# One signal per round, a fourth buffer of split rows, and one wait per block in a two-layer graph network

## The chip, the cores and the metric

The kernel runs on one core of one Trainium2 chip. The metric is the device time of one execution in microseconds. A core has five engines with queues of their own: TensorE (PE; PEld is its weight load), VectorE (DVE), ScalarE (ACT), GpSimd (POOL) and SyncE (SP). An engine works through its queue in order, and engines wait for each other through semaphores. In this kernel SyncE issues nearly all plain transfers and GpSimd the indirect ones (gathers).

## The reference

A graph of 12500 nodes with 256 features and 200000 edges, sorted by destination; destinations are skewed to low node numbers. Two layers of mean aggregation, an output product, a residual and a normalization:

```python
def _sage_conv(x, src, dst, W_l, b_l, W_r):
    msgs = x[src]
    agg = jax.ops.segment_sum(msgs, dst, num_segments=N_NODES)
    deg = jax.ops.segment_sum(jnp.ones((src.shape[0],), x.dtype), dst, num_segments=N_NODES)
    mean = agg / jnp.maximum(deg, 1.0)[:, None]
    return mean @ W_l + b_l + x @ W_r

h = jax.nn.relu(_sage_conv(x, src, dst, W1_l, b1, W1_r))
h = jax.nn.relu(_sage_conv(h, src, dst, W2_l, b2, W2_r))
return layernorm(x + h @ W3 + b3)
```

All in float32, weights 256 x 256. (A second routine, `by_sorting`, serves inputs that do not fit the first; it is built in but not run here.)

## The kernel before

The destinations are cut into blocks of 128 nodes, 98 of them (`NB`). Edges are aggregated in two ways.

The low, much hit destinations (five groups of 256 in layer 1, seven in layer 2) go the **dense** way. `count` builds a matrix of how often each source stands before each destination of the group: VectorE compares (`pick`, L661; `low`, L665; `aft`, L671), TensorE multiplies (L706, L710) into one of three PSUM buffers `count_ps`, ScalarE copies into `counts` (L712). `product` (L628) then multiplies these counts with all rows of the table. The rows are held in DRAM as three bfloat16 parts each, `x3_d` in layer 1 and `h3_d` in layer 2. For every pair of row blocks SyncE loads one buffer `rows` (L635, 384 KB; three buffers), and TensorE does 12 matmuls on it (L638). Before that, `split_rows` (L622) makes the parts of x: a load of `split_sb`, then in turns ScalarE (L617, L619) and VectorE (L618, L620), then a store (L626).

The other edges go by **gathers**. A round takes four tiles of 128 edges. GpSimd gathers their source rows with four indirect transfers (L243) into one of four buffers `got`; TensorE multiplies the four with 0/1 matrices, 32 destinations each, into four 32-row strips of one PSUM tile (L254, in the order 3, 2, 1, 0); ScalarE copies the tile (`some`, L259). One step later `summed` adds it at the right place of a ring of sums in SBUF (L265 on TensorE, L277 on VectorE; L270 and L273 for the degrees in layer 1). A gather has to wait until the strip that last read its buffer is done, four rounds back. There are 516 rounds, 269 in layer 1 and 247 in layer 2.

When a block's sums are complete, the **block** runs in pieces: its own rows are loaded (L833) and transposed (L839, after L886 for the degrees in layer 1; copied out by L842), then `sage` (L859) makes the two products (L863 with the sums, L865 with the own rows) into one of two PSUM buffers `block_ps`, and VectorE adds (L868, L869) into the one buffer `own`; ScalarE applies the relu (L871). In layer 1 the result is stored whole (L896) and in three parts (L617 to L620 again, L899). In layer 2 it is transposed, multiplied with W3 (L921), added to x (`z`, L923), normalized and stored (L934). Where the sums came from the ring, ScalarE clears that part of it (L894 in layer 1, L913 in layer 2).

The order on TensorE and GpSimd is the order in which the program is written: `layer` (L562) steps through the rounds, lets at most two blocks be under way, a piece of one at least two turns after the piece before, and fills each third of a round with dense and counting work up to a planned cost. VectorE, ScalarE and SyncE are ordered by the tile framework's scheduler, which puts an instruction in its queue when its operands and buffers are there by its own reckoning. The framework also makes all semaphores: an instruction signals if another engine has to wait for it. An instruction holds few waits of its own; further ones stand in separate instructions ahead of it, which do nothing else. `tc.add_manual_dep(later, earlier, ...)` adds a wait by hand.

Of the kernel before, what the change touches and what calls it, by code (L numbers as in the profile page):

```python
# [7 lines left out]
F32 = mybir.dt.float32  # L8
F16 = mybir.dt.float16
BF16 = mybir.dt.bfloat16  # L10
# [7 lines left out]
ACT = mybir.EngineType.Activation  # L18
PE = mybir.EngineType.PE
POOL = mybir.EngineType.Pool  # L20

P = 128
LN_EPS = 1e-5
# [24 lines left out]
def by_runs(  # L48
# [27 lines left out]
    nc = tc.nc  # L76
    N, D = x.shape
    E = src.shape[0]
    NB = -(-N // P)
    NC = D // P  # L80
    G, W = 4, 32
# [44 lines left out]
    h_d = dram.tile([NB * P, D], F32, name="h_d")  # L126
# [46 lines left out]
    part_pool = ctx.enter_context(tc.tile_pool(name="part_ps", bufs=1, space=PSUM))  # L173
    sum_pool = ctx.enter_context(tc.tile_pool(name="sum_ps", bufs=1, space=PSUM))

    REGS = 8

    class Values:
# [5 lines left out]
        def at(self, i):  # L184
            if i not in self.have:
                a = i - self.i0
                n = min(REGS, self.row.shape[1] - a)
                _, v = nc.values_load_multi_w_load_instructions(
# [27 lines left out]
    class Gathers:  # L216
# [20 lines left out]
        def gathered(self, i):  # L237

            (gr, r), g = self.rounds[i], got[i % NGOT]
            t0, n = groups[gr]  # L240
            for j in range(G):
                e = t0 + j * n + r - C0 * P
                nc.gpsimd.indirect_dma_start(  # L243
                    out=g[:, j, :D], out_offset=None, in_=self.table,
                    in_offset=bass.IndirectOffsetOnAxis(ap=src_t[:, e:e + 1], axis=0))
            if i + AHEAD < len(self.rounds):
                self.chosen[i + AHEAD] = select(*self.rounds[i + AHEAD], self.second)
            one, two = self.chosen.pop(i)
            if r == 0:
                self.part_ps = part_pool.tile([P, D + 1], F32, name="part_ps")  # L250
            part_ps, width = self.part_ps, self.width

            for j in reversed(range(G)):
                nc.tensor.matmul(part_ps[j * W:(j + 1) * W, :width], lhsT=one[:, j],  # L254
                                 rhs=g[:, j, :width], start=r == 0, stop=r == n - 1)
            if r < n - 1:
                return None
            some = chosen_pool.tile([P, D + 1], F32, name="some", bufs=2)
            nc.scalar.copy(some[:, :width], part_ps[:, :width])  # L259
            return gr, some, two  # L260
# [18 lines left out]
    with tc.tile_pool(name="setup", bufs=1) as su, \  # L279
# [140 lines left out]

        ctx.enter_context(tc.manual_schedule(engines={PE, POOL}))
        gathers_1 = Gathers(x, False)
# [20 lines left out]
        start = su.tile([P, HC], F32, name="start")  # L443
# [8 lines left out]
        for g, (c0, c1) in enumerate(spans):  # L452
            n = c1 - c0
# [46 lines left out]
        for t in range(0, HT, 32):  # L500
            n = min(32, HT - t)
# [28 lines left out]
    w1l_sb, w1r_sb = weight(w1l, "w1l_sb"), weight(w1r, "w1r_sb")  # L530
    w2l_sb, w2r_sb, w3_sb = weight(w2l, "w2l_sb"), weight(w2r, "w2r_sb"), weight(w3, "w3_sb")

    biases = consts.tile([P, 3, D], F32, name="biases")
# [3 lines left out]
    zeros = zero.unsqueeze(2).to_broadcast([P, NC, P])  # L537
# [16 lines left out]
    work = ctx.enter_context(tc.tile_pool(name="work", bufs=2))  # L554
# [73 lines left out]
    def product(g, table3, c_sb):  # L628

        ps = dense_pool.tile([P, NC, DN], F32, name="dense_ps")  # L630
        nc.tensor.matmul(ps, lhsT=zeros_b, rhs=c_sb[:, :NC, :DN], start=True, stop=False)
        for b in range(NB):
            if b % 2 == 0:
                rows = work.tile([P, 2, 3, D], BF16, name="rows", bufs=3)
                nc.sync.dma_start(rows, table3[:, b:b + 2])  # L635
            for k in range(3):
                for c in range(NC):
                    nc.tensor.matmul(ps[:, c], lhsT=rows[:, b % 2, k, c * P:(c + 1) * P],  # L638
                                     rhs=c_sb[:, b, :DN],
                                     start=False, stop=b == NB - 1 and k == 2 and c == NC - 1)  # L640
            yield COST_DENSE
        d_sb = work.tile([P, NC, DN], F32, name="d_sb", bufs=1)
        nc.scalar.copy(d_sb, ps)
        yield d_sb
# [180 lines left out]
        return whole  # L825


    def load_rows(table, n_rows, b, name):
        t = work.tile([P, D], F32, name=name)
        n = min(P, n_rows - b * P)  # L830
        if n < P:
            nc.vector.memset(t, 0.0)
        nc.sync.dma_start(t[:n], table[b * P:b * P + n, :])  # L833
        return t

    def transposed(t, ps, name, more=0):

        for c in range(NC):
            nc.tensor.transpose(ps[:, c], t[:, c * P:(c + 1) * P], ident)  # L839
        s = work.tile([P, NC * P + 1], F32, name=name)  # L840
        n = NC * P + more
        nc.scalar.copy(s[:, :n], ps.rearrange("p c l -> p (c l)")[:, :n])  # L842
        return s[:, :NC * P].rearrange("p (c l) -> p c l", l=P), s[:, NC * P:]

    def ring(b):
# [10 lines left out]
                nc.vector.tensor_add(d, d, degs[:, RN:])  # L856
                nc.scalar.copy(degs[:, RN:], zeros[0:1, 0])

    def sage(own_t, b, agg, wl, wr, bias, name):  # L859

        ps = block_pool.tile([P, 2, D], F32, name="block_ps")
        for c in range(NC):
            nc.tensor.matmul(ps[:, 0], lhsT=agg[:, c], rhs=wl[:, c], start=c == 0, stop=c == NC - 1)  # L863
        for c in range(NC):
            nc.tensor.matmul(ps[:, 1], lhsT=own_t[:, c], rhs=wr[:, c], start=c == 0,  # L865
                             stop=c == NC - 1)
        own = work.tile([P, D], F32, name="own", bufs=1)
        nc.vector.tensor_add(own, ps[:, 1], bias)  # L868
        nc.vector.scalar_tensor_tensor(own, ps[:, 0], rdeg[:, b:b + 1], own, op0=OP.mult, op1=OP.add)  # L869
        h = work.tile([P, D], F32, name=name)  # L870
        nc.scalar.activation(h, own, AF.Relu)  # L871
        return h, own

    def turned():
        t = block_pool.tile([P, 2, D], F32, name="block_ps")
        return t.rearrange("p two (a l) -> p (two a) l", l=P)

    def first_block(b, agg=None):
        x_sb = load_rows(x, N, b, "x_sb")
        of_ring = agg is None  # L880
        yield True
        ps = turned()
        if of_ring:
            overlap(b, True)
            agg, deg_row = ring(b)
            nc.tensor.matmul(ps[:, NC, 0:1], lhsT=deg_row, rhs=ones[0:1, 0:1], start=True, stop=True)  # L886
        x_t, deg = transposed(x_sb, ps, "own_t", int(of_ring))
        if of_ring:
            nc.vector.tensor_scalar(deg, deg, 1.0, None, op0=OP.max)
            nc.vector.reciprocal(rdeg[:, b:b + 1], deg)  # L890
        yield True
        h, own = sage(x_t, b, agg, w1l_sb, w1r_sb, biases[:, 0], "h")
        if of_ring:
            nc.scalar.copy(agg, zeros)  # L894
            nc.scalar.copy(deg_row, zeros[0:1, 0])
        nc.sync.dma_start(h_d[b * P:(b + 1) * P, :], h)  # L896
        s = work.tile([P, 3, D], BF16, name="parts")
        exact(h, s, own)
        nc.sync.dma_start(h3_d[:, b], s)  # L899
        yield True  # L900

    def last_block(b, agg=None):
        h_sb = load_rows(h_d, NB * P, b, "h_sb")
        of_ring = agg is None
        yield True
        if of_ring:
            overlap(b, False)
            agg, _ = ring(b)
        h_t, _ = transposed(h_sb, turned(), "own_t")
        yield True  # L910
        h2, _ = sage(h_t, b, agg, w2l_sb, w2r_sb, biases[:, 1], "h")
        if of_ring:
            nc.scalar.copy(agg, zeros)  # L913
        x_sb = load_rows(x, N, b, "x_sb")
        yield True
        h2_t, _ = transposed(h2, turned(), "own_t")
        nc.vector.tensor_add(x_sb, x_sb, biases[:, 2])
        yield True
        y = block_pool.tile([P, 2, D], F32, name="block_ps")
        for c in range(NC):  # L920
            nc.tensor.matmul(y[:, 0], lhsT=h2_t[:, c], rhs=w3_sb[:, c], start=c == 0, stop=c == NC - 1)  # L921
        z = work.tile([P, D], F32, name="z")
        nc.vector.tensor_add(z, y[:, 0], x_sb)  # L923
        stats = work.tile([P, 6], F32, name="stats")
        nc.vector.bn_stats(stats, z)
        mv = work.tile([P, 2], F32, name="mv")
        nc.vector.bn_aggr(mv, stats)
        std = work.tile([P, 1], F32, name="std")
        nc.scalar.activation(std, mv[:, 1:2], AF.Sqrt, bias=eps)
        rstd = work.tile([P, 1], F32, name="rstd")  # L930
        nc.vector.reciprocal(rstd, std)
        nc.vector.tensor_scalar(z, z, mv[:, 0:1], rstd, op0=OP.subtract, op1=OP.mult)
        n = min(P, N - b * P)
        nc.sync.dma_start(out[b * P:b * P + n, :], z[:n])  # L934
        yield True
# [16 lines left out]
def by_sorting(  # L952
# [225 lines left out]

    REGS = 8

# [137 lines left out]
```

## Time and profile before

| | |
|---|---|
| three runs | 2904.64, 2908.94, 2911.25 us; median 2908.94 |
| the profiled execution | 2910.6 us, span 2908.8 us, mean granted TensorE clock 0.914 |
| busy | PE 2394.6 us (82%), POOL 2065.3 (71%), PEld 1632.6 (56%), DVE 1471.2 (51%), ACT 1253.6 (43%) |
| transfers | 676.44 MB, mean 233 GB/s |
| gathers L243 | 2064, of 0.95 us each in the median |
| dense matmuls L638 | 7056, 976.9 us busy |
| strips L254 | 2064 products in two passes, 359.7 us busy |

In the profile's lines `out<-in` are the program's tiles, `xN` is a count, and an arrow `<-` after an idle time or in a wait names who ended it. A line of waits reads: engine and instruction, whom it waited for, total us, number of times, longest. SPq is SyncE's queue; "issue" is time in which an engine waited for nothing that the profile shows. A line of the timeline starts with the start and the duration in us. Matmuls are pipelined and their ends are modelled, so busy times of PE overlap with each other.

### The profile page before, as it was taken

The numbers are of one execution on the slowest core, as the hardware profiler recorded it, in microseconds if no ns is written. First come the engines' busy times: TensorE is split into PE (matmuls) and PEld (weight loads), VectorE is DVE, ScalarE is ACT, GpSimd is POOL, SyncE is SP. The second block draws the span as 40 slices with busy tenths as digits, with TensorE's granted clock in tenths as the row PEclk, the third lists the DMA queues.
The fourth block names the chain that finished last, engine by engine and source line by source line (L and its number), as shares of the span: only waits on it lengthen the run. The fifth ranks groups of instructions, "written<-read, shape, count | busy, mean of one in ns | idle before, by whom it ended". The sixth has DMA issues, their size and how long they took to land.

```text
span 2908.8 us, 54100 instructions
## 1 busy us (share of the span) xinstructions
PE 2394.6 (82%) x18630; PEld 1632.6 (56%) x18630; DVE 1471.2 (51%) x4350; ACT 1253.6 (43%) x2702; POOL 2065.3 (71%) x2074
## 2 busy tenths in 40 slices
PE   3475755898998999999996677877889898899995
PEld 1132323565665666666764455555666666677774
DVE  6687764664554565566564124434323333444443
ACT  0422764675675676677673014444112122222222
POOL 5777764777777777777774777777777777777772
PEclk9676767998999999999998899889999999999998
DMA  4455668877877878767864677777989989888872
GB/s 124 128 174 164 198 188 271 260 232 235 277 228 247 273 227 292 248 215 225 251 203 124 214 246 231 219 220 230 296 284 305 299 287 291 276 265 266 266 251 71
DMA packets 408133, 676.44 MB, mean 233 GB/s; under 512 B 59659, under 2 KB 266537, under 8 KB 407849
## 3 DMA queue, kind: packets, MB, share of 16 engines
q1 hardware_dynamic: 303415, 400.51, 42.5%
q0 software_dynamic: 99072, 270.66, 30.5%
q8 instruction: 149, 2.44, 0.3%
q10 hardware_dynamic: 5362, 1.72, 0.3%
q14 instruction: 135, 1.11, 0.1%
HBM read 582.80 MB, written 89.87 MB: 231 GB/s over the span
## 4 chain that ended last, share of the span: by engine, by line
PE 54%; DMA 19%; POOL 8%; issue 7%; DVE 6%; ACT 4%; DVEq 0%; SPq 0%; ACTq 0%; POOLq 0%
PE dense_ps L638 19%; POOL got L243 8%; PE part_ps L254 7%; PE block_ps L863 6%; DMA got<-h_d,src_t 5%; PE count_ps L706 5%; PE block_ps L865 5%; PE sum_ps L265 4%; DMA x_sb<-in_x_dram 3%; DMA rows<-h_d 3%; DMA rows<-x_d 3%; PE block_ps L839 2%; PE block_ps L921 2%; DMA split_sb<-in_x_dram 2%; PE sum_ps L270 2%
## 5 line engine op out<-in xcount | busy, mean ns | idle before, releaser
L243 POOL DMA_INDIRECT got<-in_x_dram,src_t x1076 | 1116.7, 1038 | 446.5 <-issue 274.2
L243 POOL DMA_INDIRECT got<-h_d,src_t x988 | 946.4, 958 | 343.1 <-issue 285.3
L638 PE MATMUL dense_ps<-counts,rows 128*128 128x256 bf16 x7056 | 976.9, 279 | 51.3 <-DMA rows<-h_d 27.7
L712 ACT CAST counts<-count_ps 128x392 f32 (+2 forms) x1052 | 717.6, 682 | 290.2 <-PE count_ps L710 174.0
L638 PEld LDWEIGHTS <-rows 128*128 128x128 bf16 x7056 | 671.3, 100 | 287.5 <-issue 88.6
L254 PE MATMUL part_ps<-got,one 128*32 128x257 f32 (+1 forms) x4128 | 359.7, 422 | 192.1 <-DMA got<-h_d,src_t 123.0
L706 PE MATMUL count_ps<-pick,low 128*128 128x392 bf16 (+2 forms) x1052 | 343.4, 354 | 57.0 <-ACT counts L712 27.0
L661 DVE TENSOR_SCALAR pick<-steps,key_t 128x686 bf16<-128x686 f16 (+2 forms) x748 | 301.4, 413 | 127.6 <-PE count_ps L706 110.2
L201 DVE TENSOR_TENSOR one<-lo_t,lane_b 128x128 f32<-128x128 bf16 x516 | 149.1, 289 | 372.7 <-PE part_ps L254 370.5
L259 ACT COPY some<-part_ps 128x257 f32<-128x257 f32 (+1 forms) x361 | 136.1, 377 | 431.4 <-PE part_ps L254 428.2
L254 PEld LDWEIGHTS part_ps<-got,one 128*32 128x32 f32 x4128 | 85.9, 111 | 323.5 <-issue 176.4
L265 PE MATMUL sum_ps<-two,some 128*128 128x128 f32 x1444 | 238.2, 290 | 0.2 <-DVE sums L277 0.2
L265 PEld LDWEIGHTS sum_ps<-two,some 128*128 128x128 f32 x1444 | 205.0, 201 | 20.5 <-issue 8.7
L277 DVE TENSOR_TENSOR sums<-sums,sum_ps 128x256 f32 x361 | 148.4, 411 | 132.6 <-PE sum_ps L265 101.9
L868 DVE TENSOR_TENSOR own<-block_ps,biases 128x256 f32<-128x256 f32 x196 | 83.0, 423 | 230.9 <-PE block_ps L865 230.2
L706 PEld LDWEIGHTS <-low 128*128 128x128 bf16 x1052 | 101.8, 100 | 152.3 <-DVE pick L661 54.2
L842 ACT COPY own_t<-block_ps 128x256 f32<-128x256 f32 (+1 forms) x294 | 110.0, 375 | 123.7 <-PE block_ps L839 121.2
L871 ACT ACTIVATE h<-own 128x256 f32<-128x256 f32 x196 | 81.4, 415 | 179.3 <-DVE own L869 179.2
L665 DVE TENSOR_TENSOR low<-low_t,lane_b 128x512 bf16<-128x512 bf16 x187 | 127.9, 684 | 21.1 <-PE count_ps L710 20.5
L710 PE MATMUL count_ps<-aft,low 128*128 128x98 bf16 x614 | 131.9, 215 | 0.0
L863 PE MATMUL block_ps<-w1l_sb,sums 128*128 128x256 f32 x352 | 113.9, 452 | 2.1 <-DVE sums L277 1.8
L863 PE MATMUL block_ps<-w2l_sb,sums 128*128 128x256 f32 x336 | 104.1, 437 | 11.3 <-DVE sums L277 11.1
(180 smaller groups left out, 2495.1 us busy)
## 6 DMA issues: line engine op xcount, KB each, us to landing
rows<-h_d SPq DMA_DIRECT2D x343, 384.0 KB
rows<-x_d SPq DMA_DIRECT2D x245, 384.0 KB
count_d<-counts SPq DMA_DIRECT2D x28, 896.0 KB
counts<-count_d SPq DMA_DIRECT2D x28, 896.0 KB
x_sb<-in_x_dram SPq DMA_DIRECT2D x194, 128.0 KB
x_d<-parts SPq DMA_DIRECT2D x98, 192.0 KB
h_d<-parts SPq DMA_DIRECT2D x98, 192.0 KB
got<-in_x_dram,src_t POOLq DMA_INDIRECT x1076
```

The source lines that it names most:

```text
L201: nc.vector.tensor_tensor(one, lo[:, a:a + n * (G - 1) + 1:n].unsqueeze(2).to_broadcast([P, G, W]), lane_b[:, :W].unsqueeze(1).to_broadcas ...
L243: nc.gpsimd.indirect_dma_start(out=g[:, j, :D], out_offset=None, in_=self.table, in_offset=bass.IndirectOffsetOnAxis(ap=src_t[:, e:e + 1], ...
L254: nc.tensor.matmul(part_ps[j * W:(j + 1) * W, :width], lhsT=one[:, j], rhs=g[:, j, :width], start=r == 0, stop=r == n - 1)
L259: nc.scalar.copy(some[:, :width], part_ps[:, :width])
L265: nc.tensor.matmul(sum_ps[:, c], lhsT=some[:, c * P:(c + 1) * P], rhs=two, start=True, stop=True)
L277: nc.vector.tensor_add(own, own, sum_ps[:, :NC])
L638: nc.tensor.matmul(ps[:, c], lhsT=rows[:, b % 2, k, c * P:(c + 1) * P], rhs=c_sb[:, b, :DN], start=False, stop=b == NB - 1 and k == 2 and ...
L661: nc.vector.tensor_scalar(r[:, :w * NB], steps[:, :w * NB], key_t[g][:, t - lo_g:t - lo_g + 1], None, op0=OP.is_equal)
L706: nc.tensor.matmul(ps[:, :(b - a) * NB], lhsT=s, rhs=r[:, a * NB:b * NB], start=True, stop=alone)
L712: nc.scalar.copy(to[:, :, bass.ds(n0 + a, b - a)], ps[:, :(b - a) * NB].rearrange("p (d s) -> p s d", s=NB))
L863: nc.tensor.matmul(ps[:, 0], lhsT=agg[:, c], rhs=wl[:, c], start=c == 0, stop=c == NC - 1)
L865: nc.tensor.matmul(ps[:, 1], lhsT=own_t[:, c], rhs=wr[:, c], start=c == 0, stop=c == NC - 1)
```

## The change

It has three named parts, and some that come with them.

- A round's four strips signal once. The first strip in order (strip 3) is made to wait for all four gathers of its round, so the others need no wait, and only the last strip's signal is used.
- A buffer `rows` is free for its next load when the first round's strips after its products are done, instead of the products themselves; there are four such buffers, not three. If those strips are not yet written when the load is, the load falls back on the wait that the framework finds.
- In `sage` the first product waits for the sums and for `own_t`, so that the four products signal once at the end; the ring is cleared after the last of them.
- The buffers: `own` has two instead of one, `z` shares them; `h_sb` shares the buffers of `split_sb`.

```diff
@@ Gathers.gathered
+            landing = []
             for j in range(G):
                 e = t0 + j * n + r - C0 * P
-                nc.gpsimd.indirect_dma_start(
+                rows = nc.gpsimd.indirect_dma_start(
                     out=g[:, j, :D], out_offset=None, in_=self.table,
                     in_offset=bass.IndirectOffsetOnAxis(ap=src_t[:, e:e + 1], axis=0))
+                landing.append(rows.ins.name)
...
             for j in reversed(range(G)):
-                nc.tensor.matmul(part_ps[j * W:(j + 1) * W, :width], lhsT=one[:, j],
-                                 rhs=g[:, j, :width], start=r == 0, stop=r == n - 1)
+                strip = nc.tensor.matmul(part_ps[j * W:(j + 1) * W, :width], lhsT=one[:, j],
+                                         rhs=g[:, j, :width], start=r == 0, stop=r == n - 1)
+
+                for name in landing:
+                    tc.add_manual_dep(strip.ins, name, LANDED, reason="rows of the other strips")
+                landing = []
+            strips.append(strip.ins.name)
@@ product
-                rows = work.tile([P, 2, 3, D], BF16, name="rows", bufs=3)
-                nc.sync.dma_start(rows, table3[:, b:b + 2])
+                rows = work.tile([P, 2, 3, D], BF16, name="rows", bufs=NROWS)
+                load = nc.sync.dma_start(rows, table3[:, b:b + 2])
+
+                if len(used) >= NROWS and used[-NROWS] < len(strips):
+                    tc.add_manual_dep(load.ins, strips[used[-NROWS]], LANDED, reason="products done")
...
+            if b % 2:
+                used.append(len(strips))
@@ transposed
-        nc.scalar.copy(s[:, :n], ps.rearrange("p c l -> p (c l)")[:, :n])
+        copied = nc.scalar.copy(s[:, :n], ps.rearrange("p c l -> p (c l)")[:, :n])
+        turned_by[name] = copied.ins.name
@@ sage
-    def sage(own_t, b, agg, wl, wr, bias, name):
+    def sage(own_t, copied, b, agg, of_ring, wl, wr, bias, name):
...
+            if c == 0:
+                tc.add_manual_dep(product.ins, copied, LANDED, reason="the other products' rows")
...
+        if of_ring:
+            zeroed = nc.scalar.copy(agg, zeros)
+            tc.add_manual_dep(zeroed.ins, product.ins.name, LANDED, reason="it signals for all")
-        own = work.tile([P, D], F32, name="own", bufs=1)
+        own = work.tile([P, D], F32, name="own")
@@ first_block, last_block
-            nc.scalar.copy(agg, zeros)
...
-        h_sb = load_rows(h_d, NB * P, b, "h_sb")
+        h_sb = load_rows(h_d, NB * P, b, "h_sb", "split_sb")
...
-        z = work.tile([P, D], F32, name="z")
+        z = work.tile([P, D], F32, name="z", tag="own")
```

`NROWS` is 4; `strips` and `used` are lists that start empty; the pool `work` has two buffers of a tile unless a number is given.

More of the change, by code (lines that the diff above doesn't have):

```diff
@@ L20 @@
 POOL = mybir.EngineType.Pool
+LANDED = mybir.DependencyInfo(mybir.DependencyClass.Sync, mybir.DependencyReason.DATA)
 P = 128
@@ L174, in by_runs @@
     sum_pool = ctx.enter_context(tc.tile_pool(name="sum_ps", bufs=1, space=PSUM))
+    strips, used = [], []
+    NROWS = 4
     REGS = 8
@@ L825, in cost_of, with load_rows @@
         return whole
-    def load_rows(table, n_rows, b, name):
-        t = work.tile([P, D], F32, name=name)
+    def load_rows(table, n_rows, b, name, tag=None):
+        t = work.tile([P, D], F32, name=name, tag=tag or name)
         n = min(P, n_rows - b * P)
@@ L834, in load_rows @@
         return t
+    turned_by = {}
     def transposed(t, ps, name, more=0):
@@ L857, in overlap @@
                 nc.scalar.copy(degs[:, RN:], zeros[0:1, 0])
-    def sage(own_t, b, agg, wl, wr, bias, name):
+    def sage(own_t, copied, b, agg, of_ring, wl, wr, bias, name):
         ps = block_pool.tile([P, 2, D], F32, name="block_ps")
         for c in range(NC):
-            nc.tensor.matmul(ps[:, 0], lhsT=agg[:, c], rhs=wl[:, c], start=c == 0, stop=c == NC - 1)
+            product = nc.tensor.matmul(ps[:, 0], lhsT=agg[:, c], rhs=wl[:, c], start=c == 0,
+                                       stop=c == NC - 1)
+            if c == 0:
+                tc.add_manual_dep(product.ins, copied, LANDED, reason="the other products' rows")
         for c in range(NC):
-            nc.tensor.matmul(ps[:, 1], lhsT=own_t[:, c], rhs=wr[:, c], start=c == 0,
-                             stop=c == NC - 1)
-        own = work.tile([P, D], F32, name="own", bufs=1)
+            product = nc.tensor.matmul(ps[:, 1], lhsT=own_t[:, c], rhs=wr[:, c], start=c == 0,
+                                       stop=c == NC - 1)
+        if of_ring:
+            zeroed = nc.scalar.copy(agg, zeros)
+            tc.add_manual_dep(zeroed.ins, product.ins.name, LANDED, reason="it signals for all")
+        own = work.tile([P, D], F32, name="own")
         nc.vector.tensor_add(own, ps[:, 1], bias)
@@ L890, in first_block @@
             nc.vector.reciprocal(rdeg[:, b:b + 1], deg)
+        copied = turned_by["own_t"]
         yield True
-        h, own = sage(x_t, b, agg, w1l_sb, w1r_sb, biases[:, 0], "h")
+        h, own = sage(x_t, copied, b, agg, of_ring, w1l_sb, w1r_sb, biases[:, 0], "h")
         if of_ring:
-            nc.scalar.copy(agg, zeros)
             nc.scalar.copy(deg_row, zeros[0:1, 0])
@@ L909, in last_block @@
         h_t, _ = transposed(h_sb, turned(), "own_t")
+        copied = turned_by["own_t"]
         yield True
-        h2, _ = sage(h_t, b, agg, w2l_sb, w2r_sb, biases[:, 1], "h")
-        if of_ring:
-            nc.scalar.copy(agg, zeros)
+        h2, _ = sage(h_t, copied, b, agg, of_ring, w2l_sb, w2r_sb, biases[:, 1], "h")
         x_sb = load_rows(x, N, b, "x_sb")
```

## The prediction

> **What bounds the kernel now.** First the page: the span, the chain that ended last, the slices.
>
> ```profile
> span 2908.8 us, 54100 instructions
> ...
> PE   3475755898998999999996677877889898899995
> ...
> PE 54%; DMA 19%; POOL 8%; issue 7%; DVE 6%; ACT 4%; DVEq 0%; SPq 0%; ACTq 0%; POOLq 0%
> ```
>
> TensorE carries the chain. It has two weak stretches: 220 to 510 us (digits 5, 7, 5, 5 from the fourth on), where counting and row splitting overlap, and the first half of layer 2 (6, 6, 7, 7 from 1530 us). By the windows the DMA engines are busy 0.92 and 0.91 between 2100 and 2500 us. Next, the waits of the first of these stretches, 300 to 530 us:
>
> ```profile
> PEld block_ps L886 <- DVE own L869: 56.6, 7, 19.4
> ...
> PE block_ps L886 <- DVE own L869: 54.3, 7, 19.1
> POOL got L243 <- PE part_ps L254: 48.4, 9, 17.9
> ```
>
> Seven times TensorE stands for a block's addition on VectorE, 54.3 us in all, and GpSimd with it. VectorE's order of time around the longest of them shows why:
>
> ```profile
> 456.93 0.42 DVE L618 TENSOR_TENSOR own<-h,parts 128x256 f32<-128x256 f32 x1
> 457.48 0.43 DVE L620 TENSOR_TENSOR parts<-split_sb,parts 128x256 bf16<-128x256 f32 x1
> 457.82 0.42 DVE L620 TENSOR_TENSOR parts<-own,parts 128x256 bf16<-128x256 f32 x1
> 458.27 0.42 DVE L868 TENSOR_TENSOR own<-block_ps,biases 128x256 f32<-128x256 f32 x1
> ...
> 464.13 0.48 DVE L869 SCALAR_TENSOR_TENSOR own<-block_ps,rdeg,own 128x256 f32<-128x256 f32 x1
> ```
>
> ```profile
> 464.66 0.58 PE L886 MATMUL block_ps<-ones,degs 1*128 1x1 f32 x2 [19.08 <-DVE own L869]
> ```
>
> There is one buffer `own`. A block's L868 can stand only behind the last reader of the block before (L620 `parts<-own`), and that one stands among the row splits (L617 to L620), which go at the pace of their loads. TensorE gets block_ps back 19.08 us late. Third, the rows of the dense products, and what SyncE's queue waits for before it loads them:
>
> ```profile
> SPq L635 <- PE dense_ps L638: 624.3, 291, 11.3
> ```
>
> ```profile
> PEld L638 <- DMA rows<-h_d: 35.7, 22, 4.4
> PEld L638 <- DMA rows<-x_d: 28.7, 17, 3.6
> ```
>
> SyncE nearly always waits for a buffer, yet TensorE waits for rows only 64.4 us.
>
> **The change, part by part**, against the profiled execution (2910.6 us, span 2908.8; median of the runs 2908.94, so 1.7 less). In the built programs TensorE and GpSimd keep their order. TensorE's signals fall from 5483 to 3161; its instructions that only wait rise from 424 to 1386; the orders of VectorE, ScalarE and SyncE move.
>
> *Two buffers of `own` (the diff's `bufs=1` goes).* Counting the blocks in their order from 0, the new VectorE order puts the L868 of blocks 3 to 12 some 7 to 23 of the 196 split instructions earlier. In this trace block 9's L868 starts at 458.3, right behind the 160th split instruction (ended 457.9); it will stand behind the 140th, ended 415.9. So the seven waits should shrink, and POOL's 48.4 us with them. But the lead is capped by the splits, which are no faster: block 12 (L868 at 544.6) will stand behind the 189th, ended 528.7: 15.9 us ahead at most; block 13 (550.2) behind all 196 as before, ended 538.9: 11.3. Ends: 11 and 54.3 us. I take 16, block 12's, since TensorE asks for a block's buffer only a block or two later. What is late next there are the splits themselves, and L706 waiting for VectorE's `pick`.
>
> *Rows: four buffers, released by the next round's strips.* 206 of the 588 loads now have no TensorE wait of their own (4 before): the pool's buffer is freed by something SyncE has seen already. For the other 382 I set the new releasing strip at its time in this trace: 203 become free later than with three buffers (0.6 us typically, up to 2.5), 179 earlier (up to 4). Walking SyncE's queue in its new order with these times and each load's own landing time, against the time TensorE wanted it: of 56.3 us of clear stalls (35 loads) 40.4 would go, and 31 other loads would come late by 24.9 in sum. Queued behind a held load are x_sb, h_sb, the output stores and the h stores; they went through the same walk and moved by under 0.1 us in the median. Net -15.5. But in layer 2 TensorE also waits 123.0 us for gathers (PE part_ps L254 <- DMA got<-h_d, 51 times), and a load that is early hands the time to the next strip. I take half, -8; ends -40 and +25.
>
> *One signal per round, 516 rounds.* In the trace's semaphore events the four increments of a round stand 42 to 43 ns apart, so who waits for the last strip is released 0.13 us sooner. Gathers wait on L254 58 times (87.4 us): at most 7.4, mostly inside the stretch counted above. TensorE itself is not held by signals:
>
> ```profile
> 703.18 0.09 PEld L270 LDWEIGHTS sum_ps<-two,some 128*1 128x1 f32 x2
> 703.49 0.55 PEld L638 LDWEIGHTS <-rows 128*128 128x128 bf16 x6 [0.22 <-issue]
> ...
> 704.47 0.16 PEld L254 LDWEIGHTS part_ps<-got,one 128*32 128x32 f32 x8 [0.20 <-issue]
> 705.04 0.10 PEld L706 LDWEIGHTS <-low 128*128 128x128 bf16 x1 [0.41 <-issue]
> ```
>
> After a round of strips the next weight load comes 0.31 us after the last pass starts, a pass being 0.22: 0.09 over. After L270, which signals once, it comes 0.20 after a pass of 0.11: the same 0.09. So the gap belongs to the change of tile shape. Take -2, ends 0 and -7. The Trainium skill (TensorE: Matmul & The Clock Gate, "The cost: per-tile semaphore tail") says that increments of packed tiles serialize and that each beyond the first lengthens the tail by 26.3 ns. An estimate by that page, were the tail to hold TensorE in each round, is 3 x 26.3 ns x 516 = 41 us faster; L270's equal gap speaks against counting it.
>
> *More instructions that only wait.* Rounds whose strips started within 0.2 us of the last gather's landing: 87. Where a separate wait stood before them (44) the start came 0.136 us after landing, elsewhere 0.044. All rounds will have it: 43 x 0.092 = 4.0. With rows long landed the gap from a dense product to the first strip is 0.20 us with and without it. The products' wait for sums becomes separate too: 23 waits (PEld L863 <- DVE sums) x 0.092 = 2. Together +6, ends 0 and +12 (the second wait instruction costing as much again).
>
> *A block's products wait for own_t at the first one, and the ring is zeroed after the last.* No line has L865 waiting for own_t; 0. The zeroing:
>
> ```profile
> ACT sums L913 <- PE block_ps L863: 168.0, 80, 8.7
> ...
> ACT sums L894 <- PE block_ps L863: 70.6, 76, 4.5
> ```
>
> ScalarE always waits there, and will wait for two products more: 0.83 us, 172 times. Behind it stand h (71 times, which needs the same products) and L712's copies of counts (87 times, 72 us). Three buffers of count_ps cover these; TensorE waits for L712 27.0 us in all. +2, ends 0 and +27.
>
> *z shares own's two buffers, h_sb the splits'.* 33 L868 now wait for an output store; in this trace two would be late, 2.3 us in sum. +2, ends 0 and +10. The signals dropped in dense products cost nothing either way: the next matmul comes 0.11 us later with or without one.
>
> Sum: -16 - 8 - 2 + 6 + 2 + 2 = -16: 2894.6 for the profiled execution, 2893 for the median.
>
> **Rivals.** *Slower: loads held for strips.* The mechanism is the late release at SyncE, in layer 2. For: 203 later releases, DMA engines nine tenths busy, a tenth of layer 2's loads land under 0.5 us before use. Price: nothing recovered and 24.9 lost puts the rows at +25 instead of -8: the sum is +17, 2926. It decides once the rows' stalls grow by more than 8 us over their 64.4. Against: 179 earlier releases, and 206 loads without a wait.
>
> *No change: the early lead is handed back.* GpSimd needs 0.95 us and 0.30 idle a gather, 2064 gathers, 2580 us; if it is the bound from 560 us on, a lead of TensorE alone melts. Against: GpSimd's own waits of 48.4 us stand in the same stretch, so it moves up too. 2909, within 6.
>
> *More than that.* The waits at L886 go nearly whole (-40) and the splits end sooner because TensorE's early start frees ScalarE; with -8, -2 and +10: -40, 2869. Against: block 13's place.
>
> **How the numbers follow.** Two runs differ by a few us; about 0.2% (6 us) can be told from no change. Forecast (faster by 6 to 30): 0.57, 2893. More: 0.12. No change: 0.12. Slower: 0.19. So faster 0.69, same 0.12, slower 0.19. The range takes the rows' ends and most of the larger gain: 2866; above, no change and part of the slower case: 2917. The likeliest case alone spans 2879 to 2903.
>
> **What would show it.** Right: L886's waits on own between 300 and 530 us fall from 54.3 to under 35, and the first dense stage ends some 16 us sooner; GpSimd's L254 waits fall there. Rows: PEld L638's waits within 64 plus or minus 20. The gap after strips stays 0.31 us; strips bound by a gather start about 0.14 us after landing. Wrong: L886's waits stay (the order on VectorE does not matter), waits for rows in layer 2 above 75 us, or the lead at 600 us gone at 2800.

## The result, and the profile after

The changed kernel is faster by 0.8%: the ratio of its time to that of before is 0.992, interval 0.9894 to 0.9947. Its profiled execution took 2887.15 us (before 2910.6), with a span of 2885.3 us and a mean granted TensorE clock of 0.921 (0.914). Two of its first four runs took 7536.89 and 9753.42 us at a granted clock of 1.0; six later runs of the same kernel (2878.76 to 2889.06 us) showed nothing of the kind, what the two were is not known, and they are left out of every number here, so that the ratio rests on the other two (2887.15 and 2879.91 us).

Page of the change: span and instructions, busy times, the 40 slices of TensorE, the chain that ended last.

```profile
span 2885.3 us, 55011 instructions
...
PE 2401.5 (83%) x18630; PEld 1633.6 (57%) x18630; DVE 1465.0 (51%) x4350; ACT 1244.9 (43%) x2702; POOL 2058.5 (71%) x2074
...
PE   4475785897998998999996778777889899999995
...
PE 53%; DMA 18%; POOL 10%; issue 7%; DVE 6%; ACT 4%; DVEq 0%; SPq 0%; ACTq 0%; POOLq 0%
```

There are 911 instructions more (the ones that only wait), and no engine is busy for longer by more than 7 us. The slices from the fourth on read 5, 7, 8, 5 where they read 5, 7, 5, 5: the gain is in the stretch in which rows are split. The waits of 300 to 530 us in the change (line L886 of before is L913 here, L868 and L869 are L895 and L896, L254 is L262, L243 is L250):

```profile
POOL got L250 <- PE part_ps L262: 35.6, 12, 20.5
...
PEld block_ps L913 <- DVE own L896: 28.8, 2, 23.0
...
PE block_ps L913 <- DVE own L896: 28.3, 2, 22.7
```

TensorE stood seven times for `own`, 54.3 us; now it stands twice, 28.3 us. A third time follows behind the end of this stretch, 8.5 us at 535 us, so over the whole run it is 54.3 against 36.7 us (the line is below). Next the windows of the same stretch, first of before, then of the change. The columns are start and end, then each engine's busy us, the granted clock, the DMA share and GB/s.

```profile
300.00:500.00 200.00, 116.52 (x703) 59.28 (x699) 129.59 (x383) 126.90 (x269) 122.37 (x117) 0.75 0.72 224
500.00:650.00 150.00, 135.48 (x1163) 91.71 (x1167) 94.15 (x276) 104.10 (x200) 106.33 (x102) 0.97 0.77 246
```

```profile
300.00:500.00 200.00, 141.97 (x854) 72.77 (x854) 133.70 (x398) 128.83 (x276) 137.93 (x131) 0.74 0.77 236
500.00:650.00 150.00, 130.91 (x1145) 87.45 (x1146) 92.76 (x273) 103.51 (x204) 101.64 (x99) 0.91 0.73 236
```

In the same 200 us TensorE ran 854 matmuls, not 703, and GpSimd issued 131 operations, not 117. The order on TensorE is the same in both kernels, so the start of its k-th matmul can be compared. The change is 3 us ahead at 300 us, 43 at 475, 26 at 500 and 512, 13 at 570 and 619, 19 at 720, 23 at 1100, 17 at 2180, 28 at 2832 and 23.5 at the end: of the 43 us, 17 are handed back by 500 us and 13 or 14 more between 512 and 570 us, the rest is kept. Two traces of before (this one and e8, below) lie up to 8 us apart at the same matmul, so single leads are good to some 8 us.

The lines that the other terms rest on, from the waits of the whole run. Before:

```profile
PE part_ps L254 <- DMA got<-h_d,src_t: 123.0, 51, 14.0
...
PE part_ps L254 <- DMA got<-in_x_dram,src_t: 57.5, 23, 6.7
```

The change:

```profile
ACT sums L892 <- PE block_ps L889: 376.3, 165, 12.7
...
PE part_ps L262 <- DMA got<-h_d,src_t: 103.0, 49, 11.5
...
PEld L654 <- DMA rows<-h_d: 54.1, 33, 6.7
...
PE part_ps L262 <- DMA got<-in_x_dram,src_t: 47.3, 22, 6.6
...
PEld L654 <- DMA rows<-x_d: 38.7, 19, 7.4
...
PE block_ps L913 <- DVE own L896: 36.7, 3, 22.7
...
DVE own L895 <- DMA out_dram<-z: 2.0, 1, 2.0
```

Waits for rows rose from 64.4 to 92.8 us, while waits for gathers fell from 180.5 to 150.3.

### The profile page after: what moved, and what is told of

It reads as the page before. It is cut to its first block, busy times and chain, and to the rows that moved or that the text cites. A ratio compares the mean times of both kernels' runs of the same rounds, so it can differ in the third digit from the quotient of the medians.

```text
span 2885.3 us, 55011 instructions
## 1 busy us (share of the span) xinstructions
PE 2401.5 (83%) x18630; PEld 1633.6 (57%) x18630; DVE 1465.0 (51%) x4350; ACT 1244.9 (43%) x2702; POOL 2058.5 (71%) x2074
## 4 chain that ended last, share of the span: by engine, by line
PE 53%; DMA 18%; POOL 10%; issue 7%; DVE 6%; ACT 4%; DVEq 0%; SPq 0%; ACTq 0%; POOLq 0%
PE dense_ps L654 19%; POOL got L250 10%; PE part_ps L262 7%; PE block_ps L884 5%; PE count_ps L724 5%; DMA rows<-h_d 5%; PE block_ps L889 4%; DMA got<-h_d,src_t 4%; PE sum_ps L278 4%; DMA x_sb<-in_x_dram 3%; DMA rows<-x_d 2%; PE block_ps L859 2%; PE block_ps L947 2%; PE sum_ps L283 1%; DMA got<-in_x_dram,src_t 1%
## 5 line engine op out<-in xcount | busy, mean ns | idle before, releaser
L250 POOL DMA_INDIRECT got<-in_x_dram,src_t x1076 | 1114.2, 1035 | 430.5 <-issue 276.4
L250 POOL DMA_INDIRECT got<-h_d,src_t x988 | 942.2, 954 | 338.9 <-issue 262.6
L262 PE MATMUL part_ps<-got,one 128*32 128x257 f32 (+1 forms) x4128 | 361.1, 423 | 161.6 <-DMA got<-h_d,src_t 103.0
L262 PEld LDWEIGHTS part_ps<-got,one 128*32 128x32 f32 x4128 | 87.3, 112 | 291.6 <-issue 245.4
L892 ACT COPY sums<-zero 128x256 f32<-128x256 f32 x172 | 69.3, 403 | 376.5 <-PE block_ps L889 376.3
L290 DVE TENSOR_TENSOR sums<-sums,sum_ps 128x256 f32 x361 | 148.3, 411 | 152.4 <-PE sum_ps L278 123.0
L895 DVE TENSOR_TENSOR own<-block_ps,biases 128x256 f32<-128x256 f32 x196 | 82.8, 423 | 244.7 <-PE block_ps L889 242.4
L683 DVE TENSOR_TENSOR low<-low_t,lane_b 128x512 bf16<-128x512 bf16 x187 | 127.7, 683 | 26.7 <-PE count_ps L728 26.3
```

Source lines behind the costliest of these rows:

```text
L250: rows = nc.gpsimd.indirect_dma_start(out=g[:, j, :D], out_offset=None, in_=self.table, in_offset=bass.IndirectOffsetOnAxis(ap=src_t[:, e: ...
L262: strip = nc.tensor.matmul(part_ps[j * W:(j + 1) * W, :width], lhsT=one[:, j], rhs=g[:, j, :width], start=r == 0, stop=r == n - 1)
L290: nc.vector.tensor_add(own, own, sum_ps[:, :NC])
```

## The experiments

Runs e1 to e4 fell on a chip on which before itself takes 3416.03 us (median of 23 runs); they are compared with before on that chip only. In e5 to e8, on a second chip, and in e9 to e12, on a third, before takes 2906 us, as it did at first; these too are compared with before on their own chip.

**Own alone (e1).** Before, with

```diff
-        own = work.tile([P, D], F32, name="own", bufs=1)
+        own = work.tile([P, D], F32, name="own")
-        z = work.tile([P, D], F32, name="z")
+        z = work.tile([P, D], F32, name="z", tag="own")
```

> The kernel before with one edit: own has two buffers, which z shares. No signal, no rows buffer and no wait of the change is in it. Theory (the second own buffer lets a block's addition go ahead of the row splits on VectorE): the waits at L886 for own between 300 and 530 us fall from 54.3 us to 20 to 35, TensorE is 12 to 18 us ahead at 600 us and keeps it: 2889 to 2897 us, 0.4 to 0.65% faster than before. Rival (the named parts, signals and released rows, bring the gain): within 4 us of before, 2903 to 2911.

Measured: 0.9935 (0.9916 to 0.9955). TensorE's waits for `own` are 34.4 us, three times, over the whole run.

**All but own (e2).** The change, with `bufs=1` for `own` and `z`, which are separate again.

> The changed kernel with a single own again, and z with one buffer of its own for want of room (z acts only in layer 2, so layer 1 is the test). All three named parts of the change stay. Theory: the waits at L886 are back (50 us and more), TensorE is at 600 us where it was before, within 4 us; layer 2 loses a few us to the single z, so 2905 to 2925 in all. Rival (named parts): TensorE is still 12 to 18 us ahead at 600 us, and L886's waits stay near 28 us.

Measured: 0.997 (0.9955 to 0.9984), where 2905 to 2925 us had meant 0.2% faster to 0.5% slower. The waits for `own` are back as expected (57.0 us, six times). With that, own did not look like the whole gain on this chip.

**The release of rows (e3).** The change without its wait by hand on the rows' load; the fourth buffer stays:

```diff
-                if len(used) >= NROWS and used[-NROWS] < len(strips):
-                    tc.add_manual_dep(load.ins, strips[used[-NROWS]], LANDED, reason="products done")
```

> The changed kernel, but the four rows buffers come free with their own products (the wait that the framework finds), not with the next strips; the dense products that end a buffer signal again (3604 TensorE signals instead of 3161). Theory A (being held for the strips makes loads late: the changed kernel waits 92.8 us for rows against 64.4 before): waits for rows fall below 50 us and the time falls by 5 to 12 us more than the change, to 2872 to 2880. Theory B (rows are not on the path, gathers are): waits for rows fall as much, those for gathers rise by the same, and the time stays within 4 us of the changed kernel's 2880 to 2887. Theory C (a signal less per product is what counts): slower than the changed kernel by over 4 us.

Measured: 0.9913 (0.9894 to 0.9932), the best median on this chip; the interval overlaps that of e1. TensorE waits for rows only 2.7 us here, against 56.8 us in e1 (three buffers) and 60.9 in e4 below (four, held for the strips). Its waits for gathers did not rise for that (22.9 us; 25.5 and 16.7). So on this chip the fourth buffer with its own release does away with the waits for rows, though little of it shows in the time of e3, which has the edits of the strips and of a block's products too. It was not run where before takes 2906 us.

**The strips' signals (e4).** The change, without the loop that makes the first strip wait for all four gathers:

```diff
-                for name in landing:
-                    tc.add_manual_dep(strip.ins, name, LANDED, reason="rows of the other strips")
-                landing = []
```

> The changed kernel with the strips as they were: each waits for its own gather and signals (4989 TensorE signals instead of 3161; 540 instructions that only wait instead of 1386). The rows' loads still wait for the last strip. Theory (single signal worth nothing in either direction: next weight load comes 0.31 us after the last pass with one signal or four, separate waits cost 92 ns only where a gather is late): within 4 us of the changed kernel. Rival 1 (a tail of signals holds TensorE: 3 x 43 ns x 516 = 66 us, or 41 us by the estimate in the prediction): 30 us and more slower than the changed kernel. Rival 2 (separate waits cost): 5 to 10 us faster, and strips bound by a gather start 0.04 us after landing where they took 0.14.

Measured: 0.9981 (0.9967 to 0.9995). That is 0.46% behind own alone (e1), which signals four times a round too, so on this chip the rows' edit or that of a block's products costs something. e3 is not behind e1: without the wait by hand that cost is gone, or the single signal makes up for it. The change itself was not run here. The trace of e1 shows that this chip says little of a kernel that waits for gathers:

```profile
POOL got L243 <- PE part_ps L254: 209.1, 73, 26.9
...
PE part_ps L254 <- DMA got<-h_d,src_t: 11.1, 1, 11.1
```

TensorE waits for layer 2's gathers once, for 11.1 us (51 times, 123.0 us, in the first trace of before), and GpSimd waits for TensorE 209.1 us, where it was 87.4. Of the two, TensorE is the later one there. So the questions were put again where before takes 2906 us.

**The change again (e5), the strips alone (e6), own and strips (e7), before for its trace (e8).** e6 is before with the two edits of the change in `Gathers.gathered`; e7 adds the edit of e1.

> The changed kernel itself on the chip of the runs it is compared with. Theory (two buffers of own give most of it, the single signal of the strips some of the rest, rows and the extra waits nothing or a loss): 0.6 to 1.0% faster than before. Rival (the strips' single signal is worth nothing and the other parts give the difference): the same ratio; this run alone does not tell them apart, it is the base for the others. If its time has a second, much longer value by its nature, some of these runs will be at 7 to 10 ms.

> Before with the strips' change alone (first strip waits for all four gathers, one signal a round; one buffer own, three rows). Theory A (signals hold nobody, the prediction's terms -2 for signals and +4 for more waits): within 0.15% of before. Theory B (a signal at each strip does hold TensorE, some 40 us in a full sum): 0.8 to 1.4% faster. Rival C (what the change gained without the strips' part and with it differ by about 0.6%): 0.5 to 0.8% faster.

> Two buffers of own (shared with z) and the strips' single signal; rows and a block's products as before. If rows and a block's products cost time in the change, this is faster than the change by 0.2 to 0.5%; if they are worth the 8 us of the prediction, it is 0.2 to 0.3% slower than the change.

> Before, unchanged, for its trace on the same chip: ratio 1 within 0.3%; TensorE's waits at L886 for own and for rows are the base for the other runs of this chip.

| | ratio to before | interval |
|---|---|---|
| e5, the change | 0.9942 | 0.992 to 0.9965 |
| e6, strips alone | 1.0005 | 0.9984 to 1.0026 |
| e7, own and strips | 0.9931 | 0.9911 to 0.9952 |

e8 took 2910.31 us once. The change lies just short of the 0.6 to 1.0% written for e5. Theory A of e6 holds: one signal a round is worth nothing that these runs resolve. The waits of e6 between 300 and 530 us are those of before (its L893 is L886):

```profile
PEld block_ps L893 <- DVE own L876: 55.2, 7, 17.3
PE block_ps L893 <- DVE own L876: 52.9, 7, 17.0
```

e7 and e5 are equal, so rows and a block's products together bring nothing and cost nothing that these runs resolve.

**Four buffers of own (e9), the change with three rows (e10), all but own again (e11), own alone again (e12).** e9 is e7 with

```diff
-        own = work.tile([P, D], F32, name="own")
+        own = work.tile([P, D], F32, name="own", bufs=4)
-        z = work.tile([P, D], F32, name="z", tag="own")
+        z = work.tile([P, D], F32, name="z", tag="own", bufs=4)
-        h_sb = load_rows(h_d, NB * P, b, "h_sb")
+        h_sb = load_rows(h_d, NB * P, b, "h_sb", "split_sb")
```

e10 is the edit of e3 on the change with `NROWS = 3`; e11 and e12 are the kernels of e2 and e1.

> Before with the strips' single signal, four buffers of own (shared with z) and h_sb in split_sb's buffers; rows and a block's products as before. VectorE's order puts the additions of blocks 6 to 14 up to 14 split operations ahead of where they stand with two buffers, and block 13 no longer behind all 196. Theory (the buffers of own set TensorE's waits at L886, and these are the gain): waits on own between 300 and 530 us fall from some 30 us with two buffers to under 15, and the time is 0.2 to 0.5% below that with two buffers, 0.8 to 1.2% below before. Rival (the row splits themselves are the cap, at the pace of their loads): the waits fall, the end of the first dense stage does not move, and the time is that of two buffers, 0.6 to 0.75% below before.

> The changed kernel with three buffers of rows that are freed by the products themselves, as before. If the fourth buffer and its release by the strips are worth the 8 us of the prediction, this is 0.2 to 0.4% slower than the change (some 0.3% faster than before). If they cost what the longer waits for rows show (8 to 28 us), it is 0.3 to 0.9% faster than the change. If the waits for rows are time that the next strip would have waited for its gathers anyway: the same as the change within 0.15%, with waits for rows back at 60 to 75 us and waits for gathers up by as much.

> The changed kernel with one buffer of own and one of z, on this chip. Theory (own is the whole gain): within 0.2% of before, waits on own at 300 to 530 us back above 50 us. Rival (the three named parts gain something by themselves): 0.25 to 0.5% faster than before.

> Before with two buffers of own, shared with z, and nothing else, on this chip. Theory: the same as the change within 0.15%, 0.55 to 0.75% faster than before. Rival: 0.2 to 0.4% slower than the change.

| | median us | ratio to before | interval |
|---|---|---|---|
| before | 2906.52 | | |
| e11, all but own | 2905.10 | 1.0003 | 0.9985 to 1.002 |
| e12, own alone, two buffers | 2885.50 | 0.9924 | 0.9896 to 0.9953 |
| e10, the change with three rows | 2884.87 | 0.9915 | 0.989 to 0.994 |
| e9, four buffers of own and z, one signal a round | 2863.53 | 0.9851 | 0.9824 to 0.9879 |

The theory of own holds, but two of the expectations missed. e9 gained more than the 0.8 to 1.2% written for it, and its waits for `own` are gone, not only under 15 us. e10's ratio (0.9915) fits that of the change (0.992 and, in e5, 0.9942), which was not run on this chip, and so the third case written for it, but its waits do not: those for rows are 89.9 us, not 60 to 75, and those for gathers 145.4, not above the change's 150.3 and (e5) 156.7. Without the second buffer the rest of the change is worth nothing that shows: in e11 the waits are back (300 to 530 us):

```profile
PEld block_ps L913 <- DVE own L896: 56.6, 7, 14.5
PE block_ps L913 <- DVE own L896: 54.3, 7, 14.2
```

With four buffers they are gone, and what is late next shows. The waits of e9 in the same stretch (its L713 is L706, L893 is L886, L258 is L254):

```profile
PEld L713 <- DVE pick L668: 38.6, 37, 3.5
...
PE count_ps L713 <- DVE pick L668: 21.7, 19, 3.2
...
POOL got L246 <- PE part_ps L258: 12.7, 8, 4.2
...
PE block_ps L893 <- DVE degs L863: 5.5, 2, 3.0
```

No line has TensorE waiting for `own`; the counting's `pick` is at the head. Windows of e9:

```profile
300.00:500.00 200.00, 153.63 (x1016) 82.84 (x1014) 145.55 (x434) 139.15 (x292) 151.94 (x145) 0.85 0.82 258
```

1016 matmuls instead of 703. e9 also gives z four buffers and lets h_sb share those of the splits, but both act in layer 2 only; at 1500 us of e8, ahead of layer 2's first gather (1590.4 us), TensorE of e9 leads e8 by 40.5 us already, and at the end by 37. So the gain is made by `own` in layer 1. e9 is the best version found: 1.5% under before, and its interval lies clear of those of e10 and e12.

## Why the prediction was right, and where it was not

The forecast, faster by 6 to 30 us, held, and so did the time (2887.15 against 2894.6 for the profiled execution). The term of own carries it. The other terms add up to 0 in the prediction (-8 - 2 + 6 + 2 + 2), and all but own changes nothing that shows in e11 (-4 to +6 us); but that 0 sets 10 us of gains, 8 of which do not show, against 10 us of costs, most of which these runs are too coarse to tell; that the sum came out is in part luck. By term:

**Two buffers of own, -16.** The mechanism is shown: it is the whole gain (e12), and without it there is none (e11). The size fits within what can be told: 0.76% of 2906.52 is 22 us, interval 14 to 30, and TensorE's waits for `own` fell by 17.6 us in the traces (54.3 to 36.7). The sign that was named, under 35 us between 300 and 530 us, was met with 28.3, but by the choice of the stretch: the third wait lies just behind it. The order on VectorE moved as the built program said. Starts of the first addition (L868) in us, and in brackets the split instructions ahead of it, from the traces:

| block | before | change | e9 |
|---|---|---|---|
| 9 | 458.3 (160) | 420.7 (140) | 384.2 (124) |
| 10 | 495.6 (174) | 468.6 (160) | 402.4 (134) |
| 12 | 544.6 (196) | 530.8 (189) | 464.1 (160) |
| 13 | 550.2 (196) | 547.2 (196) | 500.0 (174) |
| last split ends | 538.9 | 545.3 | 549.1 |

Block 9 was said to come behind the 140th split, at 415.9; it came at 420.7. Block 12 was said to come at most 15.9 us sooner; it came 13.8 sooner. With two buffers each block takes about the place of the one before it, so TensorE leads by 48 us in the trace of the change, measured against e8, until block 10's turn comes, and then it meets the same queue. VectorE of the change around that point, then TensorE:

```profile
468.16 0.42 DVE L633 TENSOR_TENSOR parts<-own,parts 128x256 bf16<-128x256 f32 x1
468.61 0.42 DVE L895 TENSOR_TENSOR own<-block_ps,biases 128x256 f32<-128x256 f32 x1
472.92 0.43 DVE L631 TENSOR_TENSOR split_sb<-split_sb,parts 128x256 f32<-128x256 f32 x1 [3.88 <-ACT parts L630]
473.26 0.48 DVE L896 SCALAR_TENSOR_TENSOR own<-block_ps,rdeg,own 128x256 f32<-128x256 f32 x1
```

```profile
473.79 0.58 PE L913 MATMUL block_ps<-ones,degs 1*128 1x1 f32 x2 [22.68 <-DVE own L896]
```

These are the prediction's lines of before again, one block on: L895 right behind `parts<-own`, L896 behind one more split that waited 3.88 us for its part, and 22.68 us of TensorE's lead gone. What the prediction had wrong here is what sets the cap. It took the pace of the splits for it. The splits were no faster (their end moved from 538.9 to 545.3 and 549.1), but e9 shows that with two buffers the buffers were still the cap: with four, block 13 stands behind 174 splits instead of 196, and 43 us are won (1.49% of 2906.52). The rival "more than that" was turned down by block 13's place. That place is a result of the buffer count, not a bound.

**Rows, -8.** This is the step that failed. Nothing of it shows: e5 has rows and a block's products beyond e7, and their medians are 2885.37 and 2887.43 us. The waits for rows rose to 92.8 us and, in e5, 83.8 (before 64.4, and 75.4 in e8), so the band of 64 plus or minus 20 was missed once, by 9 us. But with the old three buffers and the old release they are 89.9 us as well (e10), with own alone 87.1 (e12), and 99.5 in e9; in e6 and e7, also with the old buffers, they are 68.9 and 67.0. So the release by the strips is not what sets them; whether it adds something to them is not shown. Rows' (PEld) and gathers' (PE) waits behave as one account: their sum is 244.9 and 227.8 in the two traces of before, 243.1 and 240.6 in those of the change, 235.3 in e10, 247.5 in e9, while rows alone range from 64.4 to 99.5. On the slower chip they do not: there the sum falls to 25.5 us in e3, with 82.3 in e1. The walk through SyncE's queue priced each load alone; the halving for gathers that come late instead was the right thought and should have been taken whole. The same holds for the slower rival: its point of decision (stalls on rows up by more than 8 us) was passed, with 28 us, and nothing was lost. A term that may be paid in another line needs a criterion on the sum of both.

**Signals, -2, and more waits, +6.** e6 has both for the strips, and comes out at -0.16 to +0.26%, -5 to +8 us; the prediction's -2 + 4 lies inside. In the traces, 37 of 75 rounds bound by a gather in before start about 45 ns after the last landing and 37 about 135 ns; in the change 70 of 72 start at 135. The gap from the last pass of the strips to the next matmul is 312 ns in the median in both kernels. So 37 x 0.09 = 3.3 us are added, where 4.0 had been worked out. An estimate by the Trainium skill (TensorE: Matmul & The Clock Gate, "The cost: per-tile semaphore tail") had been 41 us faster, 1.4%; e6 excludes that, and the measurement decides: here the signals' tail holds no later matmul. The increments themselves stand 42 to 43 ns apart in the trace of before, against the page's 26.3.

**Ring zeroed after the last product, +2.** ScalarE's waits there rose from 168.0 + 70.6 to 376.3 us, 137.7 more, where 172 x 0.83 = 143 were worked out. Nothing came of it: e11, which has this edit, is level with before, and TensorE's waits for L712 are 30.4 us there and 29.9 in e8. (In the trace of the change they are 13.6 us against 27.0, but 10.7 of the 27.0 are one wait at 280 us, which stands there as one of 11.9 us for VectorE's `parts` instead.)

**z in own's buffers, +2.** The one wait of 2.0 us is in the lines above; 2.3 had been worked out.

**The rivals.** The lead did not melt: it is 13 us at 619 and 23.5 at the end (against e8, 17, then 10 at 1700 us, and 23 at the end), and e9's, against e8, is 37 at the end. GpSimd is not the bound that would take it back.

Left open: on the slower chip all but own gains 0.3% (e2), own alone 0.65% (e1), own with rows and products but without the strips' signal only 0.2% (e4), and the change without the rows' wait 0.9% (e3). Elsewhere these parts are worth nothing that shows (e6, e7, e10, e11). Which of them matters on the slower chip was not settled; strips alone, or the change itself, run there would tell. Nor was a fourth buffer of rows with its own release (e3) run on the others.

## What to carry to other kernels

When an engine stands for a buffer that passes through another engine's in-order queue, look at the order of that queue, not at the work in it: a buffer more moves the instruction up, and the next cap may be the same buffer again, so try the next count before naming another bound. Where two kinds of transfers are waited for in turn, judge an edit to one of them by the sum of both waits. A wait that is gone from one line may stand in another, or just behind the stretch that was looked at: compare whole runs. Signals dropped and waits merged are worth what the trace shows of held engines, here nothing that shows.

## What the runs showed of the hardware that was not expected

The same program took 2906 us on two chips and 3416 on another, 17.5% more, while the mean granted clock was 0.92 and 0.87, a difference of 6%. On the slower one (e1) a quarter of the rounds took 565 ns or more from the last strip's pass to the next matmul; on another (e8) the 75th percentile was 313 ns and the 90th 567. The medians were 312 ns on both. The granted clock is either 1.0 or 0.5 in the clock records of e1, e8 and e12, and it is 0.5 for 876 us of e1 and 436 us of e8.

This does not account for all of it. e1 and e12 are the same kernel, 3397.1 and 2883.3 us long. The clock is 0.5 for 444 us in e12, so by an estimate from these records the 432 us more in e1 cost at most half of that, 216 us of the 514. TensorE's idle time, in gaps of over 150 ns, rises by 321 us (788 against 467). Of it 229 us in e1, against 0.4 in e12, end with nothing in the profile that released TensorE. What holds it there is not known.
